# Layer 0 of a four-layer network: a table of slots for its first stage, another order within a slot, and state buffers from a free list

## The chip, the core and the metric

The kernel runs on one core of one Trainium2 chip. A core has a matrix engine (TensorE, PE in the profile; PEld is its weight load), VectorE (DVE), ScalarE (ACT), GpSimd (POOL), and SyncE (SP), which here issues the transfers between DRAM and the on-chip memory. Each engine works through its own instructions in order and waits on semaphores for the others. The metric is the device time of one execution in microseconds (us).

## The reference

Four layers follow each other on an input of 4 x 96 x 64 x 64: a Mamba block with a fusion, a convolution block, an attention with a feed-forward net, and an FFT mixer with a feed-forward net. The change touches layer 0 alone:

```python
def _mamba_block(seq, ...):            # seq: 4 x 4096 x 96
    h = layernorm(seq) * ln_g + ln_b
    xs, z = split(h @ in_w)            # 192 channels each
    xc = silu(causal_conv4(xs) + conv_b)
    dt, Bm, Cm = split(xc @ xproj_w)   # 6, 16 and 16
    delta = softplus(dt @ dt_w + dt_b)
    dA  = exp(delta[..., None] * A)    # 192 channels x 16 states
    dBx = delta[..., None] * Bm[:, :, None, :] * xc[..., None]
    # h[t] = dA[t] * h[t-1] + dBx[t], along the 4096 steps
    y = einsum('blds,bls->bld', hstates, Cm) + Dp * xc
    return (y * silu(z)) @ out_w
# twice: seq = seq + _mamba_block(seq, weights of i), then
# a 1x1 convolution with a pooled term, batch norm and the residual
```

## The kernel before

Layer 0 works on **32 items**: 4 pieces of 1024 steps (s), 2 blocks (i), 4 images (b), in the order s, i, b, so an item's input (load_x) is in_x for i = 0 and the DRAM buffer xd for i = 1, which finish of the same image and piece wrote four items earlier. Items 0 to 7 have s = 0 and start from a zero state; the others carry one.

The recurrence is a scan instruction on VectorE. The 192 channels and 16 states make 24 tiles of 128 partitions (32 channels by 4 states) and 1024 steps, one scan each: three thirds p of the channels, two halves j, and four groups g of states. One item is thus **24 slots**, one for each scan, and the list order (L512) says which (p, g, j) slot t scans. The groups get their two operands in three ways:

- g = 0, 1 ("d"): fill (L544, L549) broadcasts B into PSUM by a matmul on PE, and VectorE multiplies it by udb (L586) ahead of the scan;
- g = 2, GP: POOL multiplies udb by brep (times_b, L571), and the exponential goes to PSUM (dap);
- g = 3, GA: ScalarE weighs du by B (weigh, L451), and fill transposes it on PE into PSUM.

The factor dA is an exponential on ScalarE (exp, L560), three scans ahead for the groups other than GP (three buffers), one ahead for GP. After the second scan of a (p, g), POOL multiplies hs by crep in place (times_c, L600), keep_state (L606) copies the last column, and sum_y (L617) adds the group to y[p] by matmuls. start_y (L610) opens y[p] with D times xc, gate (L628) multiplies it by silu(z), project and project_z (L635, L246) form the output in PSUM, and finish (L647 to L661) copies it out and stores it.

hs has **four buffers**; a table keeps says which one a (p, g) takes. A buffer is free once sum_y has read it. PSUM has two 1024-wide banks (u and x) for fills, u and dap, two y banks used in turn (also by the transposes turn_du and tb), and two tiles "ps" for everything else.

The **first stage** (first_stage, L277) of an item runs as steps in the slots of the two items ahead of it. A step has a slot number t: 0 to 23 are slots of the item one ahead, -24 to -1 of that two ahead, and 24 and more are slots of the item itself. Its steps: load of x (L275), centering (8 matmuls, L299), squares and scale on ScalarE, transposes and copy to n, the convolution xc in three parts of 8 matmuls (L232) with a copy each (L356), silu of xc and, with the same table, of the z of the item before (L367, L472), xproj, dbl, the store of B and C to DRAM (cd), delta in three parts, softplus (L394), delta to DRAM (dd), du = delta times xc on POOL in place (L424), du to DRAM (ud), z in three parts, then turn_du (L433, four transposes on PE) and keep_du (L438, a copy over du that has to wait until the store ud has read it), 32 weighs, and the loads ddb, udb, crep and brep, which repeat rows of these DRAM buffers over partitions.

One loop over all slots m emits this, in a fixed order within a slot: scan, fill, exp, times_b, times_c, keep_state, then start_y, sum_y, gate, project, finish, then the steps of the first stages. On PE, VectorE, ScalarE and POOL that order is kept (manual_schedule). SP is not in that list: the order of the transfers is decided by the scheduler of the framework.

Of the kernel before, what the change touches and what calls it, by code (L numbers as in the profile page):

```python
# [20 lines left out]
T = 1024  # L21
# [26 lines left out]
NV128 = _n  # L48


class Net:
# [43 lines left out]
    def layer0(self, dram, scratch):  # L95
        tc, nc, ins = self.tc, self.nc, self.ins
        x_in = ins["x"]
        with ExitStack() as ctx:
# [64 lines left out]

            def prepare():
                with tc.tile_pool(name="l0s", bufs=1) as wk, tc.tile_pool(name="l0g", bufs=1) as sums_pool:
# [39 lines left out]
                    for m in sorted(stages[0])[:4]:  # L205
                        for f in stages[0].pop(m):
                            f()
# [70 lines left out]
            def first_stage(k):  # L278
# [5 lines left out]
                def at_slot(t):  # L284
                    def keep(f):
                        steps.setdefault(t - 24, []).append(f)

                    return keep

                @at_slot(-20)  # L290
                def _():
                    m["xn"] = load_x(b, s, i) if k else x0


                @at_slot(-11)
                def _():
                    m["ps"] = [tile_ps(128), tile_ps(128)]
                    for q in range(8):
                        nc.tensor.matmul(  # L299
                            m["ps"][q // 4][:, q % 4 * C : q % 4 * C + C],  # L300
                            m["xn"][:, q * 128 : q * 128 + 128],
                            self.center,
                            start=True,
                            stop=True,
                        )

                @at_slot(-10)
                def _():
                    if k:
                        nt = wk.tile([128, 8 * C], F32, name="nt", tag="nt")  # L310
                    else:
                        nt = first_pool.tile([128, 8 * C], F32, name="nt")
                    m["nt"] = nt[:, : 8 * C].rearrange("p (q c) -> p q c", q=8)
                    m["rs"] = cp.tile([128, 8], F32, name="rs", tag="rs")
                    for q in range(8):
                        nc.scalar.activation(
                            m["nt"][:, q],
                            m["ps"][q // 4][:, q % 4 * C : q % 4 * C + C],
                            AF.Square,
                            accum_out=m["rs"][:, q : q + 1],  # L320
                        )
                    nc.scalar.activation(m["rs"], m["rs"], AF.Ln, scale=1.0 / C, bias=self.eps)
                    nc.scalar.activation(m["rs"], m["rs"], AF.Exp, scale=-0.5)

                @at_slot(-9)
                def _():
                    for q in range(8):
                        x = m["ps"][q // 4][:, q % 4 * C : q % 4 * C + C]
                        nc.scalar.mul(m["nt"][:, q], x, m["rs"][:, q : q + 1])

                @at_slot(-7)
                def _():
                    m["ps"] = [tile_ps(), tile_ps()]
                    for q in range(8):
                        nc.tensor.transpose(
                            m["ps"][q // 4][:, q % 4 * 128 : q % 4 * 128 + 128], m["nt"][:, q], self.ident
                        )

                @at_slot(-6)
# [23 lines left out]
                parts_of("xc", [(w_x[:, i, k], k) for k in range(4)], n, ((-6, -4), (-3, -2), (0, 0)), 2)  # L363

                @at_slot(1)
                def _():
                    nc.scalar.activation(m["xc"], m["xc"], AF.Silu)  # L367
                    if k:
                        silu_z(k - 1)
                    exp_set()  # L370
# [7 lines left out]
                @at_slot(3)  # L378
# [4 lines left out]
                @at_slot(4)  # L383
# [6 lines left out]
                parts_of("delta", [(dtw[:, i], 0)], dbl, ((5, 5), (6, 6), (7, 7)), 1)  # L390

                @at_slot(7)
# [4 lines left out]
                @at_slot(8)  # L397
# [7 lines left out]
                @at_slot(9)  # L405
# [9 lines left out]
                @at_slot(8)  # L415
                def _():
                    spread_out("delta", "dd")

                @at_slot(10)
# [7 lines left out]
                parts_of("z", [(w_z[:, i], 3)], n, ((12, 12), (12, 12), (13, 13)), 2)  # L427
# [15 lines left out]
                for p in range(3):  # L443
                    at_slot(14 + p)(lambda p=p: (turn_du(p), keep_du(p)))
# [13 lines left out]
                for t, count in ((19, 4), (20, 5), (21, 5), (22, 4), (23, 6), (24, 6), (28, 2)):  # L458
# [3 lines left out]
                for p in range(3):  # L462
                    for j in range(2):
                        at_slot((15, 24, 31)[p] + j)(lambda p=p, j=j: load_d(m, p, j))
                    at_slot((16 if k else 15, 24, 30)[p])(lambda p=p: load_u(m, p))
                for g, t in ((GA, 20), (0, 23), (1, 25), (GP, 26)):
                    at_slot(t)(lambda g=g: load_c(m, g))
                at_slot(21 if k else 6)(lambda: load_b(m, GP))
# [38 lines left out]
            made = [{} for _ in items]  # L507

            d0, d1 = [(0, 0), (0, 1)], [(1, 0), (1, 1)]
            p0, p1, a0, a1 = ([(g, j)] for g in (GP, GA) for j in range(2))  # L510
            thirds = d0 + p0 + d1 + p1 + a0 + a1, d0 + p0 + a0 + d1 + p1 + a1, a0 + a1 + d0 + p0 + d1 + p1
            order = [(p, g, j) for p, third in enumerate(thirds) for g, j in third]  # L512
            fills = {2: 3, 5: 6, 6: 7, 7: 8, 10: 11, 11: 12, 14: 15, 15: 16, 16: 17, 17: 18, 20: 21, 23: 24}
# [7 lines left out]
            keeps = {(0, 0): 0, (0, GP): 1, (0, 1): 2, (0, GA): 3, (1, 0): 0, (1, GP): 1, (1, GA): 2, (1, 1): 3}  # L521
            keeps |= {(2, GA): 0, (2, 0): 3, (2, GP): 1, (2, 1): 2}
            ends = {max(t for t, x in enumerate(order) if x[:2] == (p, g)): (p, g) for p in range(3) for g in range(4)}
            sums = {4: (0, 0), 8: (0, 1), 9: (0, GP), 11: (0, GA), 13: (1, 0), 17: (1, 1), 18: (1, GP), 19: (1, GA)}
            sums |= {21: (2, GA), 22: (2, 0), 25: (2, 1), 27: (2, GP)}
            starts = {4: 0, 12: 1, 18: 2}
            gates = {13: 0, 21: 1, 29: 2}
# [45 lines left out]
            def scan(m):  # L573
# [13 lines left out]
                if j == 0:  # L587
                    at = keeps[h, g]
                    if k % 2 and at % 2:
                        at = 4 - at  # L590
                    made[k]["hs", h, g] = wk.tile([128, 2, T + 1], F32, name="hs", tag=f"hs{at}")
# [20 lines left out]
            def sum_y(k, p, g):  # L612

                for q, at in enumerate(halves):
                    for j in range(2):
# [8 lines left out]
                        )  # L624

# [38 lines left out]
            b_slots = {1: (0, 0, 1), 3: (0, 1, 0), 9: (0, 1, 1), 11: (0, 2, 0), 20: (0, 2, 1), 23: (1, 0, 0)}  # L664
# [3 lines left out]
            with tc.tile_pool(name="l0n", bufs=1) as first_pool:  # L668
                for m in sorted(stages[0])[:4]:
                    for f in stages[0].pop(m):  # L670
                        f()
                prepare()
            sel_r, sel_b, xproj, out_w, fus, gpw = (weights[k] for k in ("sel_r", "sel_b", "xproj", "out_w", "fus", "gpw"))
            wk = ctx.enter_context(tc.tile_pool(name="l0w", bufs=1))
            with tc.manual_schedule(engines=engines):
                gp = global_pool()
                first = min(stages[0])
                for m in range(first, last + 19):
                    k, t = divmod(m, NTL)
                    if 0 <= m < last:  # L680
                        scan(m)
                    if m == -12:
                        fill(0)
                    if t in fills and 0 < 24 * k + fills[t] < last and m >= 0:
                        fill(24 * k + fills[t])
                    if 0 <= m + 1 < last and on_pool(m + 1):
                        exp(m + 1)
                    if 0 <= m + AHEAD < last and not on_pool(m + AHEAD):
                        exp(m + AHEAD)
                    if t in b_slots:  # L690
                        ahead, p, j = b_slots[t]
                        if 0 <= k + ahead < len(items):
                            times_b(k + ahead, p, j)
                    for back, f in ((1, times_c), (3, keep_state)):
                        k0, t0 = divmod(m - back, NTL)
                        if 0 <= k0 < len(items) and t0 in ends:
                            f(k0, *ends[t0])
                    for k0 in range(max(k - 1, 0), min(k + 1, len(items))):
                        at = m - NTL * k0
                        if at in starts:  # L700
                            start_y(k0, starts[at])
                        if at in sums:
                            sum_y(k0, *sums[at])
                        if at in gates:
                            gate(k0, gates[at])
                        if at == 29:
                            made[k0]["x"] = load_x(*items[k0])
                        if at == 32:
                            project(k0)
                        if at == 33:  # L710
                            project_z(k0)
                        if at == 34:
                            finish(k0)
                    for k0 in range(max(k - 1, 0), min(k + 3, len(items))):
                        for f in stages[k0].get(m - NTL * k0, ()):
                            f()
# [879 lines left out]
```

## Time and profile before

| | us |
|---|---|
| median of three runs (lowest, highest) | 3862.44 (3851.75, 3872.67) |
| the profiled execution: its time | 3861.26 |
| its span, first to last instruction | 3859.4 |
| first scan of layer 0 starts, last one ends | 69.1, 2553.3 |

| busy over the span | PE | PEld | DVE | ACT | POOL |
|---|---|---|---|---|---|
| us | 3226.2 | 1468.0 | 2989.2 | 2722.0 | 2566.3 |
| share | 84% | 38% | 77% | 71% | 66% |

These shares are means over stages with different limits. Layer 0 is the first two thirds of the span, and in it VectorE is busy for about nine tenths of the time. The costliest groups of layer 0 are times_c (384 times 4180 ns on POOL), the exponentials (768, about 1.1 us each on ScalarE), and the scans (768, 2.28 to 2.35 us each on VectorE). Where the text gives the idle time of VectorE ahead of a scan by its slot, it is summed from the start and length of VectorE's instructions in the trace.

In the timelines below, the columns are start, length (us), engine, line, operation, result and operands, shapes, number of instructions merged; in brackets stands the idle time of the engine just before, and what ended it. In the waits, the columns are who waited for whom, the sum in us, the number of times, and the longest.

### The profile page before, as it was taken

What the parts mean: (1) busy time and instruction counts of PE and PEld (TensorE: products, weight loads), DVE (VectorE), ACT (ScalarE), POOL (GpSimd) and SP (SyncE); (2) the same over time, 40 slices, a digit from 0 to 9 for tenths busy, and PEclk for the clock granted to TensorE, in tenths of its full rate; (3) what the DMA queues carried; (4) which work ended last, traced back from release to release, by engine and by line L of the source; (5) the groups of instructions that cost most, each with busy time, mean ns of one, the idle gap of its engine ahead of it and who ended that gap; (6) DMA issues with size and microseconds to landing.
All of it is one profiled execution on the core that took longest, in us unless ns stands there. A gap on an engine that the chain in (4) does not pass through costs nothing. (4 is left out here: it accounts for less than half of the span.)

```text
span 3859.4 us, 46789 instructions
## 1 busy us (share of the span) xinstructions
PE 3226.2 (84%) x15326; PEld 1468.0 (38%) x15326; DVE 2989.2 (77%) x2644; ACT 2722.0 (71%) x5456; POOL 2566.3 (66%) x922
## 2 busy tenths in 40 slices
PE   7788888888888888888788888756899998999988
PEld 3232333323332333232322232226544534666643
DVE  5898888899989898998899999962473384444649
ACT  6787877888778787887788787741245686656557
POOL 1898888888888888988888998941001064534527
PEclk8898888899888898998898998757899999999999
DMA  7566555566656565665655766546200000011101
GB/s 189 146 152 163 144 150 148 148 157 160 160 142 157 137 156 145 166 153 143 155 150 145 170 156 167 142 121 209 98 1 1 1 1 6 17 34 34 39 9 58
DMA packets 171643, 446.62 MB, mean 116 GB/s; under 512 B 48756, under 2 KB 50750, under 8 KB 168064
## 3 DMA queue, kind: packets, MB, share of 16 engines
q1 hardware_dynamic: 171400, 443.64, 44.7%
q8 instruction: 121, 1.98, 0.2%
q14 instruction: 122, 1.00, 0.1%
HBM read 369.97 MB, written 73.50 MB: 115 GB/s over the span
## 5 line engine op out<-in xcount | busy, mean ns | idle before, releaser
L600 POOL TENSOR_TENSOR hs<-hs,crep 128x2048 f32<-128x2048 f32 x384 | 1597.3, 4180 | 333.2 <-DVE hs L595 248.2
L560 ACT ACTIVATE da<-ddb,nega 128x1024 f32<-128x1024 f32 x576 | 661.3, 1149 | 157.4 <-DVE hs L595 138.3
L595 DVE TENSOR_TENSOR_SCAN hs<-da,state,rep 128x1024 f32<-128x1024 f32 x288 | 667.9, 2337 | 46.8 <-PE rep L544 35.2
L571 POOL TENSOR_TENSOR up<-udb,brep 128x1024 f32<-128x1024 f32 x192 | 452.7, 2358 | 74.9 <-DMA udb<-ud 60.5
L617 PE MATMUL y<-hs,sel_r 128*32 128x512 f32 x3072 | 441.9, 650 | 25.5 <-POOL hs L600 25.5
L232 PE MATMUL ps<-n,w_x 97*64 97x512 f32 x1536 | 425.9, 699 | 0.0
L549 PE MATMUL rep<-dbl,sel_b 32*128 32x512 f32 x768 | 250.7, 730 | 175.7 <-DVE hs L595 174.6
L451 ACT ACTIVATE uta<-delta,bt 128x192 f32<-128x192 f32 x1024 | 375.3, 442 | 0.0
L595 DVE TENSOR_TENSOR_SCAN hs<-dap,state,up 128x1024 f32<-128x1024 f32 x144 | 336.3, 2335 | 39.4 <-PE y L617 16.9
L595 DVE TENSOR_TENSOR_SCAN hs<-da,state,u 128x1024 f32<-128x1024 f32 x144 | 338.1, 2348 | 21.7 <-PE y L617 6.8
L544 PE MATMUL rep<-ident,uta 128*128 128x128 f32 x1536 | 224.4, 293 | 74.4 <-DVE hs L595 73.8
L586 DVE TENSOR_TENSOR u<-udb,rep 128x1024 f32<-128x1024 f32 x192 | 236.0, 1229 | 64.1 <-PE rep L549 26.3
L560 ACT ACTIVATE dap<-ddb,nega 128x1024 f32<-128x1024 f32 x192 | 213.9, 1114 | 86.7 <-DVE hs L595 86.1
L544 PEld LDWEIGHTS rep<-ident,uta 128*128 128x128 f32 x1536 | 182.1, 150 | 169.0 <-DVE hs L595 89.2
L232 PEld LDWEIGHTS ps<-n,w_x 97*64 97x64 f32 x1536 | 133.8, 158 | 289.7 <-issue 251.2
L1154 POOL CAST hq<-y 128x1536 fp8e5<-128x1536 f16 x64 | 93.9, 1466 | 217.6 <-issue 122.6
L595 DVE TENSOR_TENSOR_SCAN hs<-da,rep 128x1024 f32<-128x1024 f32 x96 | 216.9, 2277 | 20.1 <-PE rep L544 16.7
L586 DVE TENSOR_TENSOR rep<-udb,rep 128x1024 f32<-128x1024 f32 x192 | 232.3, 1210 | 0.0
L617 PEld LDWEIGHTS y<-hs,sel_r 128*32 128x32 f32 x3072 | 62.3, 111 | 360.9 <-issue 233.9
L549 PEld LDWEIGHTS rep<-dbl,sel_b 32*128 32x128 f32 x768 | 65.1, 201 | 301.8 <-issue 164.1
L246 PE MATMUL ps<-xc,xproj 64*102 64x512 f32 x384 | 129.3, 824 | 58.0 <-ACT xc L367 58.0
L1293 POOL TENSOR_TENSOR av<-av,ec 128x780 f32<-128x780 f32 x32 | 58.7, 1836 | 133.5 <-ACT av L1290 133.5
(275 smaller groups left out, 6290.9 us busy)
## 6 DMA issues: line engine op xcount, KB each, us to landing
ddb<-dd SPq DMA_DIRECT2D x768, 128.0 KB
udb<-ud SPq DMA_DIRECT2D x768, 128.0 KB
crep<-cd SPq DMA_DIRECT2D x512, 128.0 KB
dd<-delta SPq DMA_DIRECT2D x64, 384.0 KB
band<-in_band SPq DMA_DIRECT2D x24, 1024.0 KB
ud<-delta SPq DMA_DIRECT2D x62, 384.0 KB
brep<-cd SPq DMA_DIRECT2D x128, 128.0 KB
x<-in_x SPq DMA_DIRECT2D x32, 384.0 KB
```

The source lines that it names most:

```text
L232: nc.tensor.matmul(ps[rows], w[:, 64 * p : 64 * p + 64], rhs[:, at.start + shift : at.stop + shift], start=k == 0, stop=k == len(ws) - 1, ...
L246: nc.tensor.matmul(ps, w[rows, p], x[rows, p], start=start and p == 0, stop=p == 2)
L451: nc.scalar.mul(m["uta"][:, q, :, 32 * s4 : 32 * s4 + 32].rearrange("t (p j) d -> t p j d", p=3), m["udt"][:, :, q].rearrange("t p (j d) - ...
L544: nc.tensor.transpose(x[:, q * 128 : q * 128 + 128], made[k]["uta"][:, q, 2 * h + j], self.ident)
L549: nc.tensor.matmul(x[:, at], sel_b[rows, g], made[k]["dbl"][rows, at], start=True, stop=True)
L560: nc.scalar.activation(da, made[k]["dd", h, j], AF.Exp, scale=nega[:, col : col + 1])
L571: nc.gpsimd.tensor_mul(up, made[k]["ud", p][:, j], made[k]["brep", GP])
L586: nc.vector.tensor_mul(u, made[k]["ud", h][:, j], x)
L595: nc.vector.tensor_tensor_scan(hs[:, 1:], made[k].pop(("da", t)), u, st, ALU.mult, ALU.add)
L600: nc.gpsimd.tensor_mul(hs[:, :, :T], hs[:, :, 1:], twice(made[k]["crep", g]))
L617: nc.tensor.matmul(made[k]["y", p][row : row + 32], sel_r, made[k]["hs", p, g][:, j, at], start=False, stop=True, skip_group_check=True,)
L1154: nc.gpsimd.tensor_copy(q, y2, saturate=False)
```

## The change

All slot numbers go into one table, SLOTS, with fractions that order the steps within a slot. The steps of a slot of the loop run in the order of SLOTS["seq"]: sum_y now comes ahead of fill, keep_state ahead of exp and gate behind scan. hs buffers come from a list, free, that sum_y appends to and scan takes from at its head. The list order keeps its content.

| step | slot before | slot after |
|---|---|---|
| load of x for a first stage | -20 | -18 |
| copies of xc parts 0, 1, 2 | -4, -2, 0 | -4 (-3.2), -1, -1 (-0.4) |
| matmuls of xc parts 0, 1, 2 | -6, -3, 0 | -5 (-4.4), -4, -2 (-1.6) |
| silu | 1 | -1 (-0.2) |
| xproj, copy of dbl | 3, 4 | 0, 2 |
| delta matmuls; copies | 5, 6, 7; 5, 6, 7 | 3, 3, 6; 5, 5, 6 |
| tb, bt | 8, 9 | 5, 8 |
| dd to DRAM, du and ud to DRAM | 8, 10 | 7, 9 |
| z matmuls; copies | 12, 12, 13; 12, 12, 13 | 11, 11, 12; 11, 12, 12 |
| turn_du; keep_du | 14, 15, 16; 14, 15, 16 | 14, 14, 16; 14, 15, 16 |
| weighs | 4 to 6 a slot in 19 to 24, 2 in 28 | 4 in 16, 7 in 19, 1 to 4 in 21 to 28 |
| load of x for project | 29 | 23 |
| project, project_z, finish | 32, 33, 34 | 31, 32, 35 |
| gate 0, 1, 2 | 13, 21, 29 | 13, 23, 28 |
| start_y 0, 1, 2 | 4, 12, 18 | 0, 10, 19 |
| sum_y (0, g), g = 0 to 3 | 4, 8, 9, 11 | 5, 7, 7, 11 |
| sum_y (1, g) | 13, 17, 18, 19 | 14, 16, 18, 19 |
| sum_y (2, g) | 22, 25, 27, 21 | 23, 24, 26, 20 |
| times_b (0,0) to (2,1) | 23 of the item ahead, 1, 3, 9, 11, 20 | 21 of the item ahead, 4, 5, 6, 13, 19 |

The diff, cut to its core (the loop's body becomes small functions, chosen by name):

```diff
+SLOTS = {'ln_ld': -18, ...
+ 'xc': ((-4.4, -3.2), (-4, -1), (-1.6, -0.4)),
+ 'silu': -0.2,
+ 'xproj': 0,
+ 'dbl': 2.4,
+ 'delta': ((3.8, 5.2), (3.8, 5.4), (6.4, 6.8)),
+ 'soft': 7.2,
+ 'tb': 5.4,
+ 'dd': 7.4,
+ 'bt': 8.2,
+ 'du': 9,
+ 'z': ((11, 11), (11, 12), (12.8, 12.8)),
+ 'turn': (14, 14.4, 16),
+ 'keep': (14.2, 15.2, 16),
+ 'weigh': ((16, 4), (19, 7), (21, 3), (22, 2), (23, 4), (24, 2), (25, 3), (26, 2), (27, 4), (28, 1)),
+ 'load_d': ((13.6, 15), (25.4, 27.6), (30.4, 34.8)),
+ 'load_u': (15.2, 23, 29.2),
+ 'load_c': (24, 22, 26.8, 26.4),
+ 'load_b': 20.8,
+ 'fills': {(0, 1, 0): 1, ... (1, 0, 0): 2, ... (1, 1, 0): 2, ... (2, 3, 1): 2, ...},
+ 'sums': ((5, 7, 7, 11), (14, 16, 18, 19), (23, 24, 26, 20)),
+ 'starts': (0, 10, 19),
+ 'gates': (13, 23, 28),
+ 'b': (4, 5, 6, 13, 19, 21),
+ 'ox': 23, 'px': 31, 'pz': 32, 'fin': 35, 'state': 2,
+ 'seq': ('scan', 'gate', 'start', 'end', 'keep', 'b', 'sum', 'exp', 'fill', 'stages', 'c'),
...
                     def keep(f):
-                        steps.setdefault(t - 24, []).append(f)
+                        steps.setdefault(int(t // 1) - 24, []).append((t, f))
...
-                    for m in sorted(stages[0])[:4]:
-                        for f in stages[0].pop(m):
-                            f()
+                    until(SLOTS["xc"][1][1])
                     spread_taps(2)
                     layer(1)
...
+            free = list(range(4))
...
                 if j == 0:
-                    at = keeps[h, g]
-                    if k % 2 and at % 2:
-                        at = 4 - at
-                    made[k]["hs", h, g] = wk.tile([128, 2, T + 1], F32, name="hs", tag=f"hs{at}")
+                    made[k]["slot", h, g] = free.pop(0)
+                    made[k]["hs", h, g] = wk.tile([128, 2, T + 1], F32, name="hs", tag=f"hs{made[k]['slot', h, g]}")
...
                             skip_group_check=True,
                         )
+                free.append(made[k]["slot", p, g])
...
-                    for back, f in ((1, times_c), (3, keep_state)):
...
+                    for step in SLOTS["seq"]:
+                        steps[step](m, k, t)
```

until runs, in the prologue, the steps of item 0 up to a slot: before, these were the first four slots and then the next four, which end with the matmuls of xc part 1; after, they end with silu.

## The prediction, made before the change was run

> **What bounds the kernel now.** I read the engines' busy time over stretches of the span first, then what VectorE waited for, then the timeline of two bad items. The stretch table, for item 17 of layer 0 (columns: stretch, length, busy us and count of PE, PEld, DVE, ACT, POOL, granted PE clock, DMA share, GB/s):
>
> ```profile
> 1404.00:1478.00 74.00, 63.44 (x322) 23.75 (x320) 71.83 (x41) 62.07 (x126) 67.83 (x20) 0.92 0.61 150
> ```
>
> VectorE is busy 71.8 of 74 us: this item is at its floor, and POOL (67.8) comes next. The starts of the 768 scans give the others: the first scan starts at 69.1, the last ends at 2553.3, so 32 items take 2484.2 us. Items 1, 9, 17, 25 and 27 idle VectorE by some 2.2 us each and take 71.8 (the first eight, without a carried state) or 73.4 us. Were all so, the loop would take 8 x 71.8 + 24 x 73.4 = 2336: **148 us of stall** is all that an order of work can win. By the slot whose scan waited: slot 10, 49 us (37 of it in items 3, 4, 5, 12, 18, 21); slots 15 to 21, 91 us (items 5-8, 13-16, 21-24, 29 and 0); slot 2, 8 us. The waits of VectorE from 69 to 2560 name the engines:
>
> ```profile
> DVE hs L595 <- PE rep L544: 51.9, 16, 4.7
> DVE hs L595 <- PE y L617: 29.8, 28, 4.9
> DVE u L586 <- PE rep L549: 26.3, 21, 2.1
> DVE hs L595 <- ACT x L647: 26.2, 4, 6.9
> ```
>
> **Slots 15 to 21**, in item 13 (starts 1084.3):
>
> ```profile
> 1119.89 3.46 POOL L424 TENSOR_TENSOR delta<-delta,xc 128x1536 f32<-128x1536 f32 x1 [0.57 <-DMA dd<-delta]
> ...
> 1127.38 1.13 PE L299 MATMUL ps<-center,x 96*128 96x96 f32 x8 [0.63 <-ACT z L356]
> ...
> 1128.54 0.33 SPq L275 DMA_DIRECT2D x<-in_x  x1
> ...
> 1128.97 1.24 SPq L413 DMA_DIRECT2D ud<-delta  x2
> ...
> 1135.21 0.58 ACT L438 COPY delta<-y 128x512 f32<-128x512 f32 x1 [5.83 <-DMA ud<-delta]
> ...
> 1136.76 1.91 PE L544 MATMUL rep<-ident,uta 128*128 128x128 f32 x8
> ...
> 1138.78 2.35 DVE L595 TENSOR_TENSOR_SCAN hs<-da,state,rep 128x1024 f32<-128x1024 f32 x1 [3.32 <-PE rep L544]
> ```
>
> delta times xc is done at 1123.4, but its write to DRAM leaves at 1128.97. SP's queue stood behind a load of x that waited for its buffer, which the centering matmuls freed at 1128.5. So keep_du(0) overwrites delta only at 1135, turn_du(1) and then fill 17 queue behind it on PE, and scan 17 waits. The load is that of item 16; SP's order isn't written out by hand, and this load reads an input, so it came ahead. That fits the list: in items 5-8, 13-16, 21-24 and 0 the load three items on reads in_x (5 to 8 load for 8 to 11, and so on); only 29 doesn't.
>
> **Slot 10**, in item 12:
>
> ```profile
> 1029.56 3.70 PE L635 MATMUL ps<-x,ident 96*96 96x512 f32 x4 [1.43 <-DMA x<-in_x]
> ...
> 1036.05 4.51 PE L246 MATMUL ps<-z,out_w 64*96 64x512 f32 x12
> ...
> 1040.48 1.06 PE L617 MATMUL y<-hs,sel_r 128*32 128x512 f32 x8
> ...
> 1041.72 2.35 DVE L595 TENSOR_TENSOR_SCAN hs<-dap,state,up 128x1024 f32<-128x1024 f32 x1 [6.16 <-ACT x L647]
> ```
>
> The scan takes the hs buffer that sum (0, GP) frees, and this sum stands behind project_z on PE, one slot ahead. The row names ACT; what came last was the sum, 1.2 us before. PE ran at half clock from 1029.2 to 1039.5. The six bad items all have a half-clock stretch that starts 24 to 26 us after their first scan; no other item from 1 on has one.
>
> **Part by part.** No compute instruction or DMA is added or dropped, and the order of scans is the same. Only who waits behind whom moves. I laid the new slots against a clean item's VectorE clock: 2.35 us a scan, 1.23 more where a slot has a multiply; slot 10 begins at 31.6, slot 16 at 48.8, the item ends at 73.3.
>
> *State slots from a free list.* Counting from the slot of the sum that frees a buffer to that of the scan that takes it: before, scans 10, 12 and 18 had one slot; now only 12 has (11 to 12), and scan 10 takes what (0, 1) freed in slot 7. POOL, in the new order, ends times_c (0, GP) at 27.4 (scan 4 ends at 16.7; then times_c 4.18, times_b 2.36, times_c 4.18), so sum (0, GP) runs to 28.5, project_z (12 rows, 2.8 us in item 13) to 31.3, fill 11 to about 33, against scan 11 at 33.9. The load of x for project goes to slot 23, six slots earlier, so the 1.43 us wait ahead of the half clock goes too. I take three quarters of 49: **36**. Bounds 0 and 49.
>
> A rule to weigh here. The Trainium skill, "TensorE: Matmul & The Clock Gate", Part 1, has the array's clock halved after at least one idle window of about 3.4 us. The new order leaves PE no such gap in slots 5 to 10, and the sum would be the whole 49. The row says otherwise: from 1025.80 to 1029.20 PE was busy for 2.25 of 3.40 us, and the clock halved.
>
> ```profile
> 1025.80:1029.20 3.40, 2.25 (x10) 1.00 1.01 259
> 1029.20:1039.50 10.30, 9.94 (x28) 0.50 0.98 241
> ```
>
> So short gaps can still halve it, and I keep a quarter of the stall (12 us).
>
> *delta times xc, dd and ud.* The multiply goes from behind times_c (1, 0) to ahead of it on POOL: 4.2 us earlier, ending near 35. dd now leaves SP ahead of load_d (2,1), whose four issues of some 0.46 us stood before it. turn_du(1) goes from behind fill 16 to ahead of it, which costs 2.35 us of slack. Before, the centering on PE stood behind sum (1, 0), which waits for times_c (1, 0), and the multiply stood behind that times_c on POOL, so load and write came free close together. Now the multiply leads by a whole times_c and should win SP's place: ud leaves near 35.5 and lands near 42 (6.2 us from issue to keep_du in item 13), ahead of keep_du(0) at 44. I take all **91**; if the load keeps its place, see the first rival.
>
> *xc and silu ahead.* xc2 goes from slot 0 to 22, silu from 1 to 23, xproj from 3 to 0. This is what can cost. ACT's opening of an item, counted by start-to-start times: from exp 23 at 65.6, two exps 2.1, six weighs 2.2, two evacuations 1.0, the silu block (rows of 1.28, 1.48, 1.47 and 1.28) 5.4, keep 0.1, exp 3 1.05, two weighs 0.7, keep 0.1, exp 2 1.1: 79.3 to 80.4, the end of exp 2. Scan 2 starts at 80.5. Slack is nil; before, the silu block stood behind exp 2. The cover is xc2 being ready at 70, with PE at full clock. Bounds 0 and 6 us an item (rival 2); clean items before had a wait of 0.4 to 1.4 at slot 2, for a similar reason, so I take 0.6: 32 x 0.6 = **-19**. PE's fill 3 has the same time to make: xproj waits for silu, and sum (2, GP), now ahead of the fill, for POOL at 78.5; full-speed PE ends the fill at 80.5 against 82.8.
>
> *Sums ahead of fills, keep_state a slot earlier, fills 8, 12, 17 two slots ahead, the rest of the loads.* Fills with one slot's lead can start only when their PSUM bank falls free, as before. Taken as nothing: POOL's 67.8 of 73.3 us covers; bounds -10 and +10.
>
> *The start.* In the prologue xc2 and silu of item 0 no longer wait behind the second layer's weights: ACT idled 5.62 us ahead of the third xc evacuation. Two matmul groups remain: **3** of it, bounds -3 and 6.
>
> Sum: 36 + 91 - 19 + 3 = 111. The profiled execution took 3861.3 (span 3859.4 and 1.9 around it): 3750. The median of the runs is 1.2 above it: **3751 us**.
>
> **Rivals.**
> 1. *The load of x keeps its place ahead of ud.* For it: SP's order is not in the diff. Then ud lands at some 51, fill 16 comes at 53.5 instead of 48.8: about 5 us in 13 items, 65 back, 3816.
> 2. *The opening becomes the bound (slower).* xc2's matmuls at half clock add 3.4 us and xproj's 2.6, in series with the silu block ahead of exp 2 and fill 3: 6 us in each of 32 items, 192 against 130 won elsewhere: 3924. It makes the kernel slower by over 0.5% from 4.7 us an item. For it: nearly every item has a half-clock stretch that begins some 3 us before its end. Against: the new order fills slots 20 to 22 with xc1 and xc2, and that stretch should start only after them.
> 3. *Everything clears*: 148 + 3, 3711.
>
> **Chances.** The forecast and what lies about it, 3725 to 3790: 0.58; everything clears 0.08; the load stays 0.22; the opening binds 0.12, of which 0.08 is slower, 0.04 within 0.5%. Half a per cent, 19 us, is about what a measurement can tell from no change. Some of the first rival's tail falls within it too. Faster 0.86, the same 0.06, slower 0.08. Range 3708 to 3825: it takes in the first rival and the clean case, and leaves out the opening.
>
> **What would show it.** Right: items of 72 to 74 us; no wait over 1 us at scan 10; ud leaving SP before the centering matmuls end; ACT's wait for "DMA ud<-delta" (77.9 us before) near nothing; a wait of about 0.5 us at scan 2, named dap. Wrong: scan 16 waiting for PE rep; scans 2 or 3 late by over 2 us in every item; scan 12 late by its sum.

## The result, and the profile after

The changed kernel takes **3831.74 us** in the median of five runs (3829.91 to 3835.07); the kernel before, five runs beside it, 3862.44 (3851.75 to 3873.96). The ratio is 0.9919, with a 95% interval from 0.9893 to 0.9945. It is faster, by 31 us where 111 were forecast, and the time lies above the predicted range. Both medians are those of the profiled executions within 2 us, so the two traces can be compared.

The span after is 3829.9 us. The loop of layer 0, from the first scan to the end of the last, first as one stretch and then item 12 alone (columns as in the stretch table of the prediction):

```profile
70.80:2520.30 2449.50, 2038.91 (x9969) 755.70 (x9965) 2264.55 (x1247) 1947.80 (x3800) 2139.37 (x605) 0.88 0.61 152
...
987.30:1063.50 76.20, 64.66 (x318) 23.67 (x318) 71.15 (x40) 61.23 (x123) 67.22 (x20) 0.89 0.61 156
```

The loop was 2484.2 us and is 2449.4, so it gave 34.7 (from unrounded times); the scans start 1.8 later, and what follows the last scan is 3.5 longer: 34.7 - 1.8 - 3.5 = 29.4, the difference of the spans (29.5) but for rounding. VectorE's work is the same. Before, good items of 73 us stood beside bad ones of 80; now nearly all are of one kind, from item 10 on 76.2 and 77.3 us in turn. The idle time of VectorE ahead of a scan, summed over items 1 to 31 by slot, and the time at half clock per item (mean of items 1 to 29):

| | slots 0-4 | 10 | 11 | 15-21 | all | at half clock |
|---|---|---|---|---|---|---|
| before | 26.9 | 52.7 | 0.0 | 99.1 | 201.0 | 15.7 |
| after | 26.2 | 46.8 | 50.6 | 27.1 | 174.3 | 16.8 |

So the stall of slots 15 to 21 went as forecast, and that of slot 10 came back as two: about 1.7 us at scan 10 and 0.7 to 2.6 at scan 11, in almost every item. The waits of VectorE in the loop say the same by line:

```profile
DVE hs L643 <- ACT dap L610: 66.7, 59, 8.4
DVE hs L643 <- PE rep L594: 51.0, 31, 2.6
DVE u L636 <- PE rep L599: 13.4, 32, 1.5
```

59 waits for dap (31 of them the one at scan 2, most of the others scan 10) and 31 for a fill (scan 11). Among ScalarE's waits, that for the store ud (77.9 us before) is gone, and this one has grown from 25.2:

```profile
ACT delta L411 <- PE ps L287: 84.3, 31, 2.9
```

It is the copy of delta's last third, which waits for its matmuls. The timeline of item 12 (starts 987.3) shows why, first for scan 10:

```profile
1006.14 1.66 PE L594 MATMUL rep<-ident,uta 128*128 128x128 f32 x8 [1.08 <-DVE hs L643]
1008.38 2.07 PE L599 MATMUL rep<-dbl,sel_b 32*128 32x512 f32 x4 [0.58 <-DVE hs L643]
1010.39 1.97 PE L287 MATMUL ps<-dbl,dtw 103*64 103x512 f32 x4
...
1012.41 0.59 ACT L411 COPY delta<-ps 128x512 f32<-128x512 f32 x1 [2.90 <-PE ps L287]
1013.11 1.28 ACT L449 ACT_TABLE_LOAD   x1
1014.40 1.48 ACT L449 ACTIVATE delta<-delta 128x1536 f32<-128x1536 f32 x1
1015.90 1.28 ACT L304 ACT_TABLE_LOAD   x1
...
1017.20 1.15 ACT L610 ACTIVATE da<-ddb,nega 128x1024 f32<-128x1024 f32 x1
1018.41 1.12 ACT L610 ACTIVATE dap<-ddb,nega 128x1024 f32<-128x1024 f32 x1
1019.62 2.35 DVE L643 TENSOR_TENSOR_SCAN hs<-dap,state,up 128x1024 f32<-128x1024 f32 x1 [1.71 <-ACT dap L610]
```

Fill 7 (L594) and fill 8 (L599) stand before delta's third part (L287) on PE. Fill 8 starts when scan 6 gives its PSUM bank free, 0.58 us after fill 7 ended, and takes 2.0 us at half clock, as delta's matmuls behind it do. ScalarE waits for them (2.90 us), then does the softplus with its two table loads, and only then exp 11 and exp 10. Scan 10 is late by 1.71.

This order is not new: fill 8 stood just ahead of delta's third part in the kernel before as well. Its slot is one earlier now, but its start is not, since scan 6 sets it: 21.2 us into the clean item 17 before, 21.1 us into item 12 after. What differs is how long the two take. Item 17 before (starts 1404.5):

```profile
1425.70 1.13 PE L549 MATMUL rep<-dbl,sel_b 32*128 32x512 f32 x4
1426.76 1.08 PE L232 MATMUL ps<-dbl,dtw 103*64 103x512 f32 x4
...
1433.72 1.11 ACT L560 ACTIVATE dap<-ddb,nega 128x1024 f32<-128x1024 f32 x1
1435.27 2.35 DVE L595 TENSOR_TENSOR_SCAN hs<-dap,state,up 128x1024 f32<-128x1024 f32 x1
```

There dap was ready 0.44 us before scan 10 took it. The chain from scan 6 over fill 8, delta, softplus and two exponentials to scan 10 had next to no slack, and at half clock its two steps on PE take 1.8 us more. The kernel after has a case of its own: item 5 (starts 454.1) has the same order, and PE at full clock from 470 to 485 us (in the stretch below its rows: stretch, length, PE's busy time, granted clock, DMA share, GB/s). Scan 10 is on time in it (0.1 us), and scan 11 too (0.1). Items 1 to 3, 6 and 7, which like item 5 carry no state yet, have half clock at that place, and their scan 10 is 1.7 to 1.9 us late.

```profile
475.00 1.13 PE L599 MATMUL rep<-dbl,sel_b 32*128 32x512 f32 x4 [1.09 <-DVE hs L643]
476.06 1.08 PE L287 MATMUL ps<-dbl,dtw 103*64 103x512 f32 x4
...
484.40 2.29 DVE L643 TENSOR_TENSOR_SCAN hs<-dap,up 128x1024 f32<-128x1024 f32 x1
```

```profile
470.00:485.00 15.00, 11.88 (x65) 1.00 0.67 156
```

Scan 11 in item 12:

```profile
1012.29 3.73 PE L684 MATMUL ps<-x,ident 96*96 96x512 f32 x4
1015.95 2.29 PE L665 MATMUL y<-hs,sel_r 128*32 128x512 f32 x16
1018.17 2.82 PE L301 MATMUL ps<-z,out_w 64*96 64x512 f32 x12
1020.92 1.13 PE L658 MATMUL y<-xc,dp 128*128 128x512 f32 x2
1021.89 1.04 PE L594 MATMUL rep<-ident,uta 128*128 128x128 f32 x8
1023.03 2.35 DVE L643 TENSOR_TENSOR_SCAN hs<-da,state,rep 128x1024 f32<-128x1024 f32 x1 [1.06 <-PE rep L594]
```

Fill 11 begins at 1021.89, last in a row of PE work without a gap: project, two sums, project_z, start_y. The stretches of the same item (columns as for item 5) show at what clock that row began:

```profile
1000.30:1003.20 2.90, 2.48 (x10) 0.52 0.54 165
1003.20:1006.60 3.40, 2.13 (x20) 0.99 1.04 243
1006.60:1016.80 10.20, 9.62 (x26) 0.50 0.33 78
1016.80:1027.00 10.20, 10.20 (x60) 1.00 0.50 120
```

PE was busy for 2.13 of 3.40 us, and for the next 10.2 us its clock was half, though it worked for 9.62 of them. Half-clock stretches lie in every item from 1 to 29; mostly one of 6.8 us at about 9 us after the first scan with one of 10.2 or 13.7 at 19, or a single one of 13.7 to 20.5 us that covers the same place. Item 5 has only a short one, which ends 13 us after its first scan.

### The profile page after: what moved, and what is told of

The parts are those of the page before. It is cut to its first block, busy times and chain, and to the rows that moved or that the text cites. A ratio compares the mean times of both kernels' runs of the same rounds, so it can differ in the third digit from the quotient of the medians.

```text
span 3829.9 us, 46555 instructions
## 1 busy us (share of the span) xinstructions
PE 3229.4 (84%) x15326; PEld 1475.1 (39%) x15326; DVE 2988.8 (78%) x2644; ACT 2719.1 (71%) x5456; POOL 2569.1 (67%) x922
## 3 DMA queue, kind: packets, MB, share of 16 engines
q8 instruction: 121, 1.98, 0.2%
## 5 line engine op out<-in xcount | busy, mean ns | idle before, releaser
L665 PE MATMUL y<-hs,sel_r 128*32 128x512 f32 x3072 | 455.4, 677 | 77.9 <-POOL hs L648 77.9
L594 PE MATMUL rep<-ident,uta 128*128 128x128 f32 x1536 | 242.3, 309 | 163.3 <-DVE hs L643 163.2
L287 PE MATMUL ps<-n,w_x 97*64 97x512 f32 x1536 | 347.4, 600 | 1.5 <-ACT n L401 1.5
L594 PEld LDWEIGHTS rep<-ident,uta 128*128 128x128 f32 x1536 | 195.7, 158 | 268.5 <-DVE hs L643 148.8
L599 PE MATMUL rep<-dbl,sel_b 32*128 32x512 f32 x768 | 247.4, 723 | 27.8 <-DVE hs L643 27.0
L636 DVE TENSOR_TENSOR u<-udb,rep 128x1024 f32<-128x1024 f32 x192 | 235.7, 1227 | 39.6 <-DMA udb<-ud 13.7
L287 PE MATMUL ps<-dbl,dtw 103*64 103x512 f32 x384 | 174.4, 960 | 74.5 <-ACT dbl L441 74.5
L287 PEld LDWEIGHTS ps<-n,w_x 97*64 97x64 f32 x1536 | 110.1, 137 | 232.8 <-issue 206.2
L479 POOL TENSOR_TENSOR delta<-delta,xc 128x1536 f32<-128x1536 f32 x31 | 106.6, 3438 | 94.4 <-DMA dd<-delta 87.7
```

The source lines that it names most:

```text
L287: nc.tensor.matmul(ps[rows], w[:, 64 * p : 64 * p + 64], rhs[:, at.start + shift : at.stop + shift], start=k == 0, stop=k == len(ws) - 1, ...
L479: (nc.gpsimd if k else nc.vector).tensor_mul(m["du"], m["delta"], m["xc"])
L594: nc.tensor.transpose(x[:, q * 128 : q * 128 + 128], made[k]["uta"][:, q, 2 * h + j], self.ident)
L599: nc.tensor.matmul(x[:, at], sel_b[rows, g], made[k]["dbl"][rows, at], start=True, stop=True)
L636: nc.vector.tensor_mul(u, made[k]["ud", h][:, j], x)
L665: nc.tensor.matmul(made[k]["y", p][row : row + 32], sel_r, made[k]["hs", p, g][:, j, at], start=False, stop=True, skip_group_check=True,)
```

## The experiments

The question after the result was which of the two sets the new stall: the order (fill 8 before delta) or the clock. Ratios are against the kernel before, run beside each on the same chip.

**Delta's third part ahead of fills 7 and 8.** One number of the table after:

```diff
- 'delta': ((3.8, 5.2), (3.8, 5.4), (6.4, 6.8)),
+ 'delta': ((3.8, 5.2), (3.8, 5.4), (5.6, 6.8)),
```

> The changed kernel with one number moved: the matmuls of delta's third part come right behind tb in slot 5, ahead of fills 7 and 8, instead of behind fill 8 in slot 6. Theory A (fill 8 waits for scan 6 to free its PSUM bank, the third part of delta waits behind it on a PE at half clock, and softplus, exp 11 and exp 10 follow it on ACT): ACT's wait for the delta matmuls (84 us) falls below 20, scan 10's wait (46.8 us over items 1 to 31) below 10, scan 11 keeps part of its 50; 3750 to 3785 us. Rival B (the half clock alone makes PE late, whatever the order): scan 10 keeps over 30 us of its wait; 3820 to 3840 us.

Measured: 3752.62, ratio 0.9703 (0.9665 to 0.9742). VectorE's idle falls from 174.3 to 105.0; scan 10 is on time in all items, scan 11 loses 11.8 in place of 50.6, and scan 7 loses 14.8, which is new. But the half clock fell too, to 8.4 us an item, since delta now fills a gap of PE. What order and clock do apart is seen in item 21 (starts 1623.8), one that has a half-clock stretch where the kernel after has them:

```profile
1641.30:1655.00 13.70, 13.70 (x44) 0.50 0.65 168
```

```profile
1641.73 1.98 PE L287 MATMUL ps<-dbl,dtw 103*64 103x512 f32 x4
...
1643.64 1.97 PE L594 MATMUL rep<-ident,uta 128*128 128x128 f32 x8
...
1651.99 1.12 ACT L610 ACTIVATE dap<-ddb,nega 128x1024 f32<-128x1024 f32 x1
...
1655.32 2.33 DVE L643 TENSOR_TENSOR_SCAN hs<-dap,state,up 128x1024 f32<-128x1024 f32 x1
...
1659.71 2.35 DVE L643 TENSOR_TENSOR_SCAN hs<-da,state,rep 128x1024 f32<-128x1024 f32 x1 [2.06 <-PE rep L594]
```

The matmuls of delta run at the same half speed (1.98 us for 4), but ahead of fill 7 (the row behind them), and dap is ready 2.2 us before scan 10 takes it. Scan 11 is late by 2.06 as before. So with delta first the chain to scan 10 has slack for the slow clock, and scan 11 has none. That takes nothing from what item 5 shows: the order that this run improves on is that of the kernel before too. Scan 7's new wait comes where fill 7 stands behind delta at half clock (items 4, 7 and 22 to 26, some 1.8 us each).

**PE kept busy, the order untouched.** The kernel after, with work done again into the same places (delta's first two thirds, and tb three times), to fill the gaps of PE in slots 4 to 6:

```diff
+for t in (5.45, 5.45, 6.1):
+    at_slot(t)(again)          # the 8 transposes of tb
+@at_slot(4.2)
+def _():
+    for p in range(2):
+        spread([(dtw[:, i], 0)], dbl, p, m["delta", p])
```

> The changed kernel with more PE work in the gaps of slots 4 to 6: delta's first two parts are computed twice in place, tb four times in place (about 3.8 us more of PE an item, same results). Theory A2 (the PE clock halves because PE has gaps there): the half-clock stretch at 18 to 30 us of an item (10 to 14 us in each) shrinks below 5 us, waits at scans 10 and 11 (97 us in items 1 to 31) fall by a third or more; 3790 to 3825 us. Rival (the clock is no cause, only the order on PE and ACT is): the added work makes PE later; 3835 us or more.

Measured: 3801.37, ratio 0.9828 (0.9798 to 0.9858); half clock 11.3 us an item; scans 10 and 11 lose 36.0 and 29.7. 16 of the items 1 to 29 still have a stretch that begins 20 us or more after the first scan, and that separates them. Stretches of PE in item 10 (starts 835.9; scans 10 and 11 late by 2.3 and 1.8) and in item 11 (starts 913.5; late by 0.2 and 0):

```profile
857.00:867.20 10.20, 10.15 (x32) 0.51 0.25 64
...
931.00:945.00 14.00, 13.56 (x90) 1.00 0.53 137
```

At full clock the order of the kernel after has no stall, at either scan, as in its own item 5. Scan 10 is thus late only where half clock meets a chain without slack, and taking away one of them is enough. Added work made the kernel 30 us faster: PE's busy time in the loop rose from 2038.9 to 2076.7, and the loop fell from 2449.5 to 2422.1.

**Where the gap comes from.** xproj moved from slot 3 to slot 0, so PE has less to do in slots 3 to 5: in item 12, 2.13 us of the 3.40 ahead of the fall of the clock. The kernel after with it back at slot 2, and what follows it:

```diff
- 'xproj': 0, 'dbl': 2.4, 'delta': ((3.8, 5.2), (3.8, 5.4), (6.4, 6.8)),
+ 'xproj': 2, 'dbl': 3.4, 'delta': ((4.2, 5.2), (4.2, 5.4), (6.4, 6.8)),
```

> The changed kernel with xproj in slot 2, behind fill 3, instead of slot 0, the copy of dbl in slot 3 instead of 2, and delta's first two parts in slot 4 instead of 3; the third part stays behind fill 8. Theory F (what lowers the clock at 18 to 30 us of an item is the gap of PE ahead of fill 6, 13 to 16 us into it, which xproj's move to slot 0 opened): the gap fills, half-clock time falls from 16.8 to below 10 us an item, the waits at scans 10 and 11 (97 us over items 1 to 31) to below 40; 3765 to 3800 us. Rival (delta's third part behind fill 8 is enough by itself, at any clock): scan 10 keeps over 30 us; 3815 us or more.

Measured: 3779.41, ratio 0.9769 (0.9719 to 0.9819). Half clock 12.2 us an item; scans 10 and 11 lose 18.2 and 28.7, about half of what they did. The time is in the range expected; half clock and waits fall less than expected (below 10 and 40). The move of xproj (with dbl and delta behind it) is a cause, and not shown to be the only one.

**Both: xproj late and delta early** (third part of delta at 5.6 in the diff above).

> The same, with delta's third part ahead of fills 7 and 8 as well. Theories A and F: nothing is left at scan 10 and below 10 us at scans 7 and 11 (27 us with delta's third part moved alone); 3730 to 3752 us, the fastest so far. Rival (later delta makes fill 7 late, as the early dbl did): scan 7 waits over 30 us; 3765 us or more.

Measured: **3740.68** (3736.83 to 3749.17), ratio 0.9678 (0.9637 to 0.972), faster than both kernels. Idle 92.2, half clock 8.5; scans 7 and 11 lose 14.9 together, where less than 10 was expected. Its loop and the waits of VectorE in it:

```profile
65.90:2429.40 2363.50, 1942.04 (x9968) 711.95 (x9964) 2260.16 (x1247) 1943.93 (x3800) 2139.78 (x605) 0.93 0.63 158
```

```profile
DVE hs L643 <- ACT dap L610: 20.0, 31, 8.4
DVE u L636 <- PE rep L599: 13.3, 31, 1.6
DVE hs L643 <- PE rep L594: 12.1, 18, 1.9
```

dap is down to the 31 waits that scan 2 has anyway, the fills from 51.0 to 12.1. Clock granted 0.93 in place of 0.88, with the same number of matmuls.

**The other way to close the gap failed.** dbl a slot earlier and the weighs that stand before it pushed back:

```diff
- 'dbl': 2.4,
+ 'dbl': 1.4,
- 'weigh': (..., (25, 3), (26, 2), (27, 4), (28, 1)),
+ 'weigh': (..., (27, 6), (28, 4)),
```

> The changed kernel with the copy of dbl on ACT ahead of five of the weighs (slot 1 instead of 2; those weighs go to slots 3 and 4). Theory E (PE's wait of about 2.3 us for dbl, 7 to 9 us into an item, starts the first half-clock stretch, and this the second one at 18 to 30): half-clock time falls from 16.8 us an item to below 8, waits at scans 10 and 11 (97 us over items 1 to 31) below 40; 3765 to 3800 us. Rival (the gaps of PE at 13 to 19 us start the second stretch, whatever came before): the half-clock time stays above 12 us and the time within 10 us of the changed kernel, 3822 to 3842.

Measured: 3841.56, ratio 0.9937 (0.9916 to 0.9959), no gain on the kernel after. The early stretch went in most items, but one begins at 13 to 16.5 us and lasts 13.7 to 17.1; in most items PE had been idle for over 3.1 of the 3.4 us before it. Scans 10 and 11 lose 47.8 and 53.2. The gap was moved, not closed. With delta early on top:

> The changed kernel with both: delta's third part ahead of fills 7 and 8, and dbl ahead of five weighs. Theories A and E together: half-clock time below 6 us an item, waits at scans 7 and 11 (27 us with the first alone) below 12; 3735 to 3752 us, below the first alone. Rival (what is left with the first alone does not come from the clock): 3750 to 3760.

Measured: 3797.28, ratio 0.982 (0.9786 to 0.9853), a miss of some 45 us. Scan 10 is on time and scan 11 loses 9.7, but scan 7 loses 55.8: the gap now lies ahead of fill 6, and fills 6 and 7 run at half clock.

**The parts of the change, alone on the kernel before.** The free list of hs buffers:

```diff
-at = keeps[h, g]
-if k % 2 and at % 2:
-    at = 4 - at
+at = made[k]["slot", h, g] = free.pop(0)
...
+free.append(made[k]["slot", p, g])
```

> The kernel before with the free list for the hs buffers and nothing else. Theory D (slot 10's wait is the sum behind project_z, but fill 11 stands behind the same project_z): slot 10 falls from 53 to below 10, slot 11 rises from 0 to 20 to 40; 3835 to 3855 us. Rival (the buffer alone cost slot 10's wait): slot 11 stays near 0; 3810 to 3820 us.

Measured: 3825.62, ratio 0.9895 (0.9861 to 0.9929), some 10 us better than expected. Slot 10 falls from 52.7 to 1.6, slot 11 rises from 0 to 19.6, the idle in all from 201.0 to 162.7.

The load of x for project six slots earlier, and du (with its stores) a slot earlier:

```diff
-@at_slot(10)
+@at_slot(9)
...
-if at == 29:
+if at == 23:
```

> The kernel before with two steps moved and nothing else: the load of x for project from slot 29 to 23, and du with its store ud from slot 10 to 9. In the compiled order of SP this puts ud ahead of the load of x in every item. Theory C (the load of x ahead of ud on SP was the cause of all waits at slots 15 to 21): ACT's wait for ud (77.9 us) falls below 10, the waits at slots 17 and 18 (79 us in items 1 to 31) below 15; 3770 to 3795 us. Rival (the order of turn_du and fill on PE matters, not SP): slots 17 and 18 keep over half; 3830 us or more.

Measured: 3807.42, ratio 0.9845 (0.9814 to 0.9876), 12 us short of the expectation. Slots 17 and 18 fall from 79 to 19, ScalarE's wait for ud is gone, slot 10 falls to 3.7; but slot 15 loses 59.2. That comes from one sum on PE, (1, 0). It in item 12 (starts 988.6), then it and scan 15 in item 13 (starts 1061.5):

```profile
1028.58 1.07 PE L617 MATMUL y<-hs,sel_r 128*32 128x512 f32 x8 [2.40 <-POOL hs L600]
...
1103.63 1.93 PE L617 MATMUL y<-hs,sel_r 128*32 128x512 f32 x8 [3.96 <-POOL hs L600]
...
1112.87 2.35 DVE L595 TENSOR_TENSOR_SCAN hs<-da,state,rep 128x1024 f32<-128x1024 f32 x1 [5.91 <-PE rep L544]
```

du now leads times_c (1, 0) on POOL by 3.4 us, and sum (1, 0) waits on PE with the fills behind it. Item 12 waits 2.40 us, keeps full clock behind it and loses 0.1 us at scan 15. Item 13 waits 3.96 us, falls to half clock, where the sum takes 1.93 us in place of 1.07, and loses 5.9. Only items with a half-clock stretch that begins 32 to 42 us after their first scan lose more than 0.1 (0.6 to 6.2). Sum (1, 0) a slot later, on top of this:

```diff
-sums = {..., 13: (1, 0), ...}
+sums = {..., 14: (1, 0), ...}
```

> The kernel before with the load of x for project in slot 23, du in slot 9, and sum (1, 0) in slot 14 instead of 13. The third edit takes the 3.3 us wait for POOL off PE ahead of z and centering, but in the compiled order of SP a load of x stands ahead of ud again. Theory C (that place on SP costs the time): the wait at scan 15 (59 us in the run without the third edit) goes below 10, and ACT's wait for ud comes back above 40 us, with waits at scans 15 to 18 wherever x is read from in_x; 3805 to 3840 us. Rival (SP's order is harmless): no wait for ud; 3740 to 3770.

Measured: 3894.81, ratio 1.0083 (1.0052 to 1.0115), slower than expected. Slot 15 is cured (1.2), but SP's order turned: a load of x stands right ahead of ud again, in every item from 0 to 30, ScalarE waits 167.6 us for it in 28 items, and slots 16 to 18 lose 146. Only the load of x earlier, without du:

> The kernel before with the load of x for project in slot 23 instead of 29 and nothing else; SP still has a load of x ahead of ud. Theory G (PE's wait for this load, 1.4 us in item 12, started the half-clock stretch at 24 us in six items): scan 10's wait (53 us over items 1 to 31) falls below 15 while the waits at scans 17 and 18 (79 us) stay above 50; 3810 to 3830 us. Rival (the buffer of one slot alone makes scan 10 late): scan 10 keeps over 35 us; 3845 to 3870 us.

Measured: 3906.28, ratio 1.0101 (1.0051 to 1.0151), well outside the expectation. Slot 10 falls to 4.5, as foreseen. But in every item from 0 to 30 the moved load itself now stands on SP right ahead of ud, as in item 10 (starts 862.7):

```profile
897.39 3.46 POOL L424 TENSOR_TENSOR delta<-delta,xc 128x1536 f32<-128x1536 f32 x1
...
904.71 1.13 PE L299 MATMUL ps<-center,x 96*128 96x96 f32 x8 [0.62 <-ACT z L356]
...
905.88 0.33 SPq L275 DMA_DIRECT2D x<-in_x  x1
906.30 1.24 SPq L413 DMA_DIRECT2D ud<-delta  x2
...
912.03 0.58 ACT L438 COPY delta<-y 128x512 f32<-128x512 f32 x1 [5.32 <-DMA ud<-delta]
```

delta is ready for the store at 900.9; ud leaves at 906.30, right behind a load that waits for the centering matmuls. Slots 17 and 18 lose 152.6. Last, the kernel after with du back behind times_c (1, 0):

```diff
- 'du': 9,
+ 'du': 11,
```

> The changed kernel with du behind times_c (1, 0) on POOL again (slot 11), all else kept; ud stays ahead of the next load of x on SP. Theory C (the load's place was the cause, du's own place a lesser one): ud leaves some 4 us later, no waits over 15 us in sum at scans 15 to 18; 3825 to 3845 us. Rival (du's earlier place on POOL is what cured slots 15 to 21): waits of 40 us or more come back at scans 16 to 18; 3865 us or more.

Measured: 3834.29, ratio 0.9914 (0.988 to 0.9948), as the kernel after. ud stays ahead of the load of x; slots 15 to 17 lose 2.2 us in all, and slot 18 its 7.0 as in the kernel after. So du's early place neither costs nor wins anything there; what counts is the order on SP.

## Why the prediction was right on the store and wrong at slot 10

**Slots 15 to 21: right.** It took 91 us; measured were 72 in items 1 to 31 (99.1 to 27.1) and 9 in item 0: 81. In item 13 (starts 1063.5), the one that showed the fault before:

```profile
1098.08 3.43 POOL L479 TENSOR_TENSOR delta<-delta,xc 128x1536 f32<-128x1536 f32 x1 [3.27 <-DMA dd<-delta]
...
1101.53 1.24 SPq L468 DMA_DIRECT2D ud<-delta  x2
...
1105.73 2.02 PE L354 MATMUL ps<-center,x 96*128 96x96 f32 x16 [0.44 <-ACT z L411]
...
1111.97 0.59 ACT L493 COPY delta<-y 128x512 f32<-128x512 f32 x1 [0.48 <-DMA ddb<-dd]
```

ud leaves 0.02 us after the multiply and 4.2 us ahead of the centering, and keep_du no longer waits for it. A load of x stood right ahead of ud on SP in 15 items before, and stands so in none after. The reason given was only half right: the multiply's early place was to win SP's order, but du back at 11 keeps that order, and on the kernel before the load moved alone does not bring it (du alone was not tried). The first rival (the load keeps its place) fell for this kernel; on the kernel before with the load moved, a load of x does stand ahead of ud.

**Slot 10: wrong, the step that failed.** "I take three quarters of 49: 36", with bounds of 0 and 49. Slots 10 and 11 went from 52.7 to 97.4, a loss of 45, so this one term is 81 us off. Two premises under it did not hold. "The new order leaves PE no such gap in slots 5 to 10": xproj's move to slot 0, costed for ScalarE alone, thins PE's work in slots 3 to 5, and the half clock that follows lies over slots 6 to 9. And the times were sums of full-speed rows with hardly any room: fill 11, put at 33 us, ends at 35.6 in item 12, and the clean item 17 starts scans 10 and 11 at 30.7 and 33.0 us, not at 31.6 and 33.9. The free list did take away what it was said to: no scan 10 waits for its hs buffer any more. But two others stood close behind it: dap, ready 0.44 us ahead of scan 10 in item 17 before, and fill 11, which ends 0.1 us ahead of scan 11 in item 5 after, both at full clock. The prediction costed neither at half clock.

**Fills two slots ahead: taken as nothing, and nothing shows against it.** Such a fill can start when its bank falls free, as before: fill 8 does so, at the same time and in the same place ahead of delta's third part as in the kernel before. Slots 12 and 17, which the other two serve, wait no longer than before (7.4 and 7.4, 45.0 and 0). Fill 8 put back by itself was not tried. Delta moved past fills 7 and 8 brought 79 us (3831.74 to 3752.62), partly through the clock, but that is an order which neither kernel had.

**Opening: mis-sized, in the safe direction.** 19 us of loss were taken; slots 0 to 4 lost nothing in items 1 to 31 (26.9 to 26.2), and item 0 some 3 us (5.9 to 8.7). The slower rival, xc2 and silu as the bound, did not show. **The start**: +3 taken, -1.8 measured.

The sum with what was measured, slots 15 to 21, slots 10 and 11, and the opening: 81 - 45 - 2 = 34 us, against 34.3 less idle of VectorE in the loop (219.3 to 185.0). The rule weighed in the prediction (the Trainium skill, "TensorE: Matmul & The Clock Gate", Part 1: half clock after an idle window of about 3.4 us) would not have found the gap either: here the clock fell after PE was busy for 2.13 of 3.40 us. The prediction saw that in one row of before and then still looked for gaps in the slots 5 to 10 only.

**Not settled.** Which edit of the table keeps ud ahead of the load of x on SP. Load and du together do on the kernel before, and stop doing so when sum (1, 0) moves by a slot; the load alone doesn't; after, it stays with du moved back. The order comes out of the framework's scheduler, and no single edit was found to decide it. Nor is it known how the 79 us of the first experiment divide between slack and clock. Moving xproj back took away about half of the new stall; what else thins PE's work there was not taken apart.

## What to carry to other kernels

Before a wait is counted as won, ask what comes ready next, and with how much slack: here a chain over PE and ScalarE stood 0.44 us behind it, and a slower PE used that up. An instruction that waits for a buffer holds up what stands behind it on its engine, and then the next engine: follow that to its end, and move what is urgent ahead of it. When work is moved away from a place on PE, look at what is left there: a thinned stretch of 3 us put the next 10 us at half speed, and the queue at the end of these 10 us pays. The place of a DMA in its queue belongs among the things to read off a trace after every edit, since an edit elsewhere can turn it.

## What the runs showed of the hardware

- The PE clock was halved after stretches that were far from idle (2.13 busy of 3.40 us in the kernel after). In items 1 to 29 the half clock then held for 3.4 to 20.5 us, and PE's work did not end it soon: in item 21 of the first experiment it held for 13.7 us in which PE was busy throughout. What does end it is not shown.
- More matmuls can take less time: 991 more of them in the loop, and a loop 27 us shorter.
- Half clock costs nothing of itself. Delta's matmuls took twice their time in item 21 of the first experiment and scan 10 was not late; whether a stretch costs is a matter of the slack of what is queued at its end.
- From item 10 on the items fell into a rhythm of two, 76.2 and 77.3 us, mostly each with its own place of the half-clock stretch, though the work of all is nearly the same.
